# Side work in queued steps of one engine, and expert products in 16-bit parts

## The chip, the cores and the metric

The kernel runs on one core of a Trainium2 chip. A core has five engines with a queue of instructions each: TensorE (PE, with its weight loads shown apart as PEld), VectorE (DVE), ScalarE (ACT), GpSimd (POOL) and SyncE (SP, which here issues DMA transfers). An engine takes its instructions in order; between engines, semaphores order the work. Matrix products land in PSUM, which DVE and ACT can read; POOL works in SBUF.

The metric is the device time of one execution in microseconds. Before the change it is 1541.74 us, the median of three runs (1539.69 to 1550.02).

## The reference

Four layers run one after the other on x of shape (2, 1024, 128), each normalised and added to a residual stream. The first two are the ones that change. The first is attention with 8 heads; the second routes each token to 2 of 8 experts and adds a shared expert:

```python
Q = (x @ Wq.T).reshape(b, n, H, R)            # H = 8, R = 64
K = (x @ Wk.T).reshape(b, n, H, R)
V = (x @ Wv.T).reshape(b, n, H, d)            # d = 128
attn = softmax(einsum('bnhr,bmhr->bhnm', Q, K))
out = einsum('bhnm,bmhd->bnd', attn, V)       # summed over heads
...
scores = softmax(xt @ gate_w.T)
top_vals, idx = top_k(scores, 2)
xs = xt[:, None, :] * weights[:, :, None]     # the token times its score
for e in range(8):
    mask = (idx == e)
    h  = silu(xs @ w1[e].T + b1[e])
    x2 = h @ w2[e].T + b2[e]
    x3 = xs @ w3[e].T + b3[e]
    y  = y + sum(x2 * x3 * mask)
z = silu(xt @ sw1.T) * (xt @ sw2.T) @ sw3.T   # shared, inner size 256
return y + z
```

The third layer is attention with 16 heads and a linear position bias, the fourth two layers of windowed attention with feed-forward parts. The kernel computes every expert for every token; the score of an expert that a token did not choose is zero.

## The kernel before

**Precision.** A product of float32 operands is made from two parts of each operand, a high one (the value rounded to a shorter type) and a low one (the rest). Three products of parts replace one (`mm3`, lines 48 to 50): high × high, high × low, low × high. The first layer uses float16 parts, the expert stage float32r parts.

**First stage** (`phase1`, from line 177). Eight pairs (two batches, four pairs of heads) of 16 steps each make 128 steps, and the loop over m runs them. A step computes scores of 128 keys for 512 queries and two heads (L300, 8 matmuls into a PSUM tile `big`), their exponentials on ACT (L304), the high part on ACT (L306) and the low part on POOL (L307). Row maxima are computed 12 steps ahead: a matmul (L269) and a reduction on DVE (L272). Nine steps behind, `values` multiplies the exponentials of eight steps with V (24 matmuls, L48 to L50) into one of two PSUM tiles in turn, `pu` and `sm`, and one step later `accumulate` divides and adds on DVE (L328, L331, L333). Every 16 steps the next pair's projections, with parts on ACT and DVE (L157/L158, L214/L215), go in between.

**Order of the work.** `queue(f)` issues a piece of work behind the last instruction recorded on each engine, so that queued work runs in the order of the program; a scheduler orders what is not queued. The main pieces of the first stage are queued. Preparation for a later stage is written as a generator; `tick()` runs it to its next `yield`. In the first stage it is called at m = 72, 76, 82, 86, 92 and at every second m from 101. One such step uses several engines, among them: loading and splitting the expert weights (ACT L429, POOL L430), `biases` with a transfer of b3 (L507 to L513), normalising the tokens (`ln_stats` on DVE with a power on POOL, L80 to L87; applied on ACT, L116), transposing them (PE L164), and `gates` (softmax of the gate, ranks, scores, L458 to L499).

**Expert stage** (`phase2`, from line 403). For each batch come two halves of the shared expert (e = −2, −1), then eight experts: 20 units over 1024 tokens each, with the channels on partitions. `stage_a` multiplies the transposed tokens with the scores, which a DMA of 512 KB broadcasts to all partitions (`fetch`), and splits the result (DVE L556, ACT L558, POOL L559). `stage_b` makes the first and third products (one matmul per 512 tokens with the bias b3 as an outer product with the mask, L580), silu on ACT (L575), and splits h (ACT L582, DVE L583). `stage_c` makes the second product, y = (p + b2) · x3 on DVE (L600) and adds it to yT on DVE or POOL in turn (L601). None of these is queued. Three PSUM tiles `big` of two banks are shared by all products. `finish` transposes yT back, normalises and adds it to X (L609, L610). From i = 13 two ticks per unit prepare the third stage.

```python
if m in (72, 76, 82, 86, 92) or m >= 101 and m % 2 == 0:
    k.queue(k.tick)
```

Of the kernel before, what the change touches and what calls it, by code (L numbers as in the profile page):

```python
# [22 lines left out]
NT = N // 128  # L23
# [6 lines left out]
class Core:  # L30


    def __init__(self, tc, A):
        self.tc, self.nc, self.A = tc, tc.nc, A
        self.last = {}

# [100 lines left out]
    def add_ln_steps(self, pool, X, src, T, t0):  # L137

        mv, rstd = self.ln_stats(pool, src, T)
        yield  # L140
        y = pool.tile([128, T, D], F32, name="ln_y")
        self.ln_to(pool, [y[:, t, :] for t in range(T)], src, mv, rstd, True)
        yield
        self.nc.vector.tensor_tensor(X[:, t0 : t0 + T, :], X[:, t0 : t0 + T, :], y, ALU.add)
# [32 lines left out]
def phase1(k, X):  # L177
# [9 lines left out]
    with ExitStack() as es:  # L187
# [31 lines left out]
        def tokens(b):  # L219
            xn = tp.tile([128, NT, D], F32, name="xn")  # L220
            xTh, xTl = x2.tile([128, N], F16, name="xTh"), x2.tile([128, N], F16, name="xTl")
            for c in range(2):
                src = X[:, NT * b + 4 * c : NT * b + 4 * c + 4, :]
                mv, rstd = k.ln_stats(x2, lambda t: src[:, t, :], 4, False)
                yield
                k.ln_to(x2, [xn[:, 4 * c + t, :] for t in range(4)], lambda t: src[:, t, :], mv, rstd, scalar=b == 1)
                s = slice(512 * c, 512 * c + 512)
                yield
                hi, _ = k.split_r(xTh[:, s], xTl[:, s], k.transposed(ps_sm, xn, c))
                S["first"] = S.get("first", hi)  # L230
            S["x", b] = xTh, xTl

# [77 lines left out]
        def values(n):  # L310
# [4 lines left out]

            S["u", n] = po = ps_u.tile([128, D + 1], F32, name="pu") if n % 2 else ps_sm.tile([128, D + 1], F32, name="sm")
# [5 lines left out]
        def accumulate(n):  # L322
# [11 lines left out]
            if h == H - 1 and i == 7:  # L334
                args = X, lambda t: acc[:, 4 * c + t, :], 4, NT * b + 4 * c
                if b == 0 or c == 0:
                    S["finish"] = k.add_ln_steps(xp, *args)
                else:
                    k.later.append(lambda pool: k.add_ln(pool, *args, scalar=True))
# [21 lines left out]
        for m in range(steps + lag + 1):  # L361
# [8 lines left out]
            if m == 100:  # L370
                projecting.close()
# [3 lines left out]
            if 0 <= m - lag - 1 < steps:  # L375
                k.queue(accumulate, m - lag - 1)
            if "finish" in S and m % 2:
                k.queue(next, S["finish"], None)
            if 0 <= m - lag < steps:
                k.queue(values, m - lag)  # L380
            if m % 8 == 4 and m + 4 < steps:
# [3 lines left out]
            if m == 22:  # L385
                more = tokens(1)
            if m in (22, 26, 30, 36, 42):
                k.queue(next, more, None)
# [4 lines left out]
            if m in (72, 76, 82, 86, 92) or m >= 101 and m % 2 == 0:  # L393
                k.queue(k.tick)


def np_halves(w):

    v = w.rearrange("p t d -> p (t d)")
    return [v[:, 512 * i : 512 * i + 512].rearrange("p (t d) -> p t d", d=64) for i in range(2)]  # L400


def phase2(k, X):

    nc, A = k.nc, k.A
    E = 8
    with ExitStack() as es:
        pool = lambda name, bufs: es.enter_context(k.pool(name, bufs, "right"))
        sp = pool("p2s", 1)
        gp = pool("p2g", 1)  # L410
        dp = es.enter_context(k.tc.tile_pool(name="p2d", bufs=2, space=bass.MemoryType.DRAM))
# [3 lines left out]
        work = lambda: gp.tile([128, NT, 128], F32, name="work")  # L415
# [5 lines left out]
        b2 = lambda e: gb[:, 2 * E + e : 2 * E + e + 1]  # L421
        W = {}

        def load(pool, n, m, raw, split=nc.vector):
            w = raw[:, :m, :]
            nc.sync.dma_start(w, A["t_" + n])
            yield
            h, l = pool.tile([128, m, D], F32R, name=n + "h"), pool.tile([128, m, D], F32R, name=n + "l")
            nc.scalar.copy(h, w)  # L429
            split.tensor_tensor(l, w, k.f(h), ALU.subtract)  # L430
            W[n] = h, l

        S = {}

        def tokens(b, xp):

            Xb = X[:, NT * b : NT * b + NT, :]
            mv, rstd = k.ln_stats(gp, lambda t: Xb[:, t, :])
            yield
            xn = work()  # L440
            xT = xp.tile([128, N], F32, name="xT")
            xTh = xp.tile([128, N], F32R, name="xTh")
            xTl = xp.tile([128, N], F32R, name="xTl")
            S[b] = xT, xTh, xTl
            k.ln_to(gp, [xn[:, t, :] for t in range(NT)], lambda t: Xb[:, t, :], mv, rstd, scalar=True)
            yield
            for c in range(2):
                s = slice(512 * c, 512 * c + 512)
                ps = k.transposed(ps_sm, xn, c)
                nc.scalar.copy(xT[:, s], ps)  # L450
                k.split_r(xTh[:, s], xTl[:, s], xT[:, s])
                yield

        def gates(b, xp):
# [3 lines left out]
            for t in range(NT):  # L458
                nc.tensor.matmul(ps[:, t, :], xT[:, 128 * t : 128 * t + 128], gwT, start=True, stop=True)
            m = gp.tile([128, NT], F32, name="m")  # L460
# [3 lines left out]
            nc.vector.tensor_tensor(lg, ps, bc(m), ALU.subtract)  # L464
            ex = gp.tile([128, NT, E], F32, name="ex")
# [7 lines left out]
            cmp, c2 = (work_.rearrange("p t (i e) -> p t i e", e=E) for work_ in np_halves(work()))  # L473
            mine = sc.unsqueeze(3).to_broadcast([128, NT, E, E])
            other = sc.unsqueeze(2).to_broadcast([128, NT, E, E])
            nc.vector.tensor_tensor(cmp, other, mine, ALU.is_gt)
            nc.vector.tensor_tensor(c2, other, mine, ALU.is_equal)
            yield
            nc.vector.tensor_tensor(c2, c2, k.tri.unsqueeze(1).to_broadcast([128, NT, E, E]), ALU.mult)
            nc.vector.tensor_tensor(cmp, cmp, c2, ALU.add)  # L480
            rank = gp.tile([128, NT, E], F32, name="rank")
            nc.vector.tensor_reduce(rank, cmp, AX.X, ALU.add)
            rows = work()
            nc.gpsimd.memset(rows, 0.0)
            for o in (0, 32):
                nc.vector.tensor_scalar(rows[:, :, o : o + E], rank, 1.5, None, ALU.is_lt)
            nc.vector.tensor_tensor(rows[:, :, 64 : 64 + E], sc, rows[:, :, 0:E], ALU.mult)
            yield
            rT = xp.tile([128, N], F32R, name="rT")
            sT = gp.tile([128, N], F32, name="sT")  # L490
            for c in range(2):
                s = slice(512 * c, 512 * c + 512)
                ps = k.transposed(ps_sm, rows, c)
                nc.scalar.copy(rT[0:64, s], ps[0:64, :])
                nc.scalar.copy(sT[64 : 64 + E, s], ps[64 : 64 + E, :])
                yield
            sd = dp.tile([E, N], F32, name="sd")
            nc.sync.dma_start(sd, sT[64 : 64 + E, :])
            S[b] += rT, sd  # L499


        b3n = sp.tile([128, D], F32, name="b3n")
        b3r = sp.tile([128, D], F32R, name="b3r")
        b3s = sp.tile([128, E, D], F32R, name="b3s")

        def biases():
            nc.gpsimd.memset(b3n, 0.0)  # L507
            nc.sync.dma_start(b3n[0:E, :], A["L0_ffn_b3"])
            nc.sync.dma_start(b3n[32 : 32 + E, :], A["L0_ffn_b3"])
            nc.vector.tensor_copy(b3r, b3n)  # L510
            nc.vector.tensor_tensor(b3r[32:64, :], b3n[32:64, :], k.f(b3r[32:64, :]), ALU.subtract)
            bc = lambda ap, d: ap.unsqueeze(d).to_broadcast([128, E, D])
            nc.vector.tensor_tensor(b3s, bc(k.f(b3r), 1), bc(k.bsel, 2), ALU.mult)  # L513

        for n in ("sw", "w1", "w3"):
            yield from load(sp, n, 6 if n == "sw" else E, work(), nc.gpsimd)
            yield
        biases()
        x0 = pool("p2x", 1)
        yield  # L520
# [7 lines left out]
        op = pool("p2o", 2)  # L528
        wp = pool("p2w", 1)
        x1 = pool("p2y", 1)  # L530
        def outs(b):
            S[b] += (xp.tile([128, N], F32, name="yT"),)

        wl = lambda n, i: (W[n][0][:, i, :], W[n][1][:, i, :])

        def product(ps, w, hi, lo, start=True):
            for c in range(2):
                s = slice(512 * c, 512 * c + 512)
                k.mm3(ps[:, c, :], *w, hi[:, s], lo[:, s], start=start)
# [4 lines left out]
        def fetch(b, e):  # L544
            if e >= 0:
                sb = tile_of("sb")
# [3 lines left out]
        def stage_a(b, e):  # L550
            xT, xTh, xTl = S[b][:3]
            if e < 0:
                S["x", b, e] = xTh, xTl
                return
            xs = tile_of("xs")
            nc.vector.tensor_tensor(xs, xT, S.pop(("s", b, e)), ALU.mult)  # L556
            xh, xl = tile_of("xh", F32R, bufs=3), tile_of("xl", F32R, bufs=3)
            nc.scalar.copy(xh, xs)  # L558
            S["xl"] = nc.gpsimd.tensor_tensor(xl, xs, k.f(xh), ALU.subtract)  # L559
            S["x", b, e] = xh, xl  # L560

        def stage_b(b, e):
            xh, xl = S.pop(("x", b, e))
            p1, p3 = big(), big()
            h = tile_of("h")
            hh, hl = tile_of("hh", F32R), tile_of("hl", F32R)
            x3 = tile_of("x3")
            if e < 0:
                product(p1, wl("sw", e + 2), xh, xl)
                S["silu"] = nc.scalar.activation(x3, flat(p1), AF.Silu)  # L570
                product(p3, wl("sw", e + 4), xh, xl)
                nc.vector.tensor_tensor(h, flat(p3), x3, ALU.mult)
            else:
# [1007 lines left out]
```

## Time and profile before

| | |
|---|---|
| median of three runs | 1541.74 us (1539.69 to 1550.02) |
| the profiled execution, its own time | 1537.82 us |
| its span in the profile | 1536.0 us |
| first stage, first to last exponential | 31.1 to 454.12 us |
| last accumulation of the first stage ends | 473.04 us |
| expert stage, last addition to yT ends | 626.86 us |
| first row maximum of the third stage | 649.2 us |
| DVE busy in the expert stage, 475 to 627 us | 138 of 152 us |
| mean granted TensorE clock | 0.899 |

All times within the execution count from the start of its span. The page gives the busy time of each engine and the costliest groups of instructions: line and engine, the names written and read with their shapes, how often, then busy time and mean duration, then the idle time of the engine just before them and what ended it ("releaser"). An idle time is put down to the event that came last. The span is 1.8 us shorter than the execution's own time. A matmul's record is longer than its share of the engine's time, since matmuls overlap.

### The profile page before, as it was taken

The page shows a single profiled execution, that of the slowest core. Times are in us where ns is not written, and L with a number is a line of the kernel's source. Part 1 is how long each engine was busy: PE and PEld are TensorE (multiplying, and loading weights), DVE is VectorE, ACT ScalarE, POOL GpSimd, SP SyncE. Part 2 cuts the span into 40 slices and gives each one's busy share as a digit, 9 for nine tenths or more (in the row PEclk, how much of TensorE's full clock was granted, in tenths as well). Part 3 has the DMA queues.
Part 4 walks back from the last instruction along what each step waited for, and adds up shares of the span by engine and source line. Part 5 has one row for each costly group of instructions (what it writes and reads, how often), then busy time and mean ns, then how long its engine had stood idle before and what let it go on. Part 6 is the DMA issues. An engine that isn't in the chain of part 4 may idle for free.

```text
span 1536.0 us, 28795 instructions
## 1 busy us (share of the span) xinstructions
PE 1229.4 (80%) x11579; PEld 785.4 (51%) x11579; DVE 1135.5 (74%) x2159; ACT 951.1 (62%) x1405; POOL 882.6 (57%) x523
## 2 busy tenths in 40 slices
PE   4899999997887887688998578864778779668785
PEld 1466665665665654444544244432555556445564
DVE  6676667766647899797888968485869669569755
ACT  2877787776755755158787558952456446456544
POOL 1766666676564456436766837674656566446521
PEclk7999999999998989689999889985889889889897
DMA  2000000000002030000001010014686745546641
GB/s 68 1 1 2 1 2 1 15 16 2 1 16 96 15 106 33 7 3 5 4 5 35 18 48 6 1 18 92 109 141 125 143 83 109 103 81 121 130 77 40
DMA packets 178433, 72.27 MB, mean 47 GB/s; under 512 B 160091, under 2 KB 169323, under 8 KB 178299
## 3 DMA queue, kind: packets, MB, share of 16 engines
q1 hardware_dynamic: 176395, 69.15, 21.7%
q8 instruction: 91, 1.49, 0.4%
q10 hardware_dynamic: 1472, 1.09, 0.2%
q0 software_dynamic: 432, 0.20, 0.1%
q14 instruction: 43, 0.35, 0.1%
HBM read 21.64 MB, written 2.16 MB: 15 GB/s over the span
## 4 chain that ended last, share of the span: by engine, by line
DVE 38%; PE 34%; ACT 11%; DMA 7%; issue 5%; POOL 3%; SPq 2%; POOLq 0%; DVEq 0%; ACTq 0%
DVE mx L806 6%; PE big L300 4%; DVE nm L272 3%; PE sm L48 2%; PE pu L857 2%; PE sm L50 2%; PE sm L49 2%; ACT pt L835 2%; DVE X L153 2%; DMA oT<-o 1%; DMA hc<-X 1%; DVE ln_st L80 1%; DMA hx<-X 1%; PE pu L48 1%; DVE ss L1133 1%
## 5 line engine op out<-in xcount | busy, mean ns | idle before, releaser
L307 POOL TENSOR_TENSOR hl<-p,hl 128x1024 f16<-128x1024 f32 x128 | 272.4, 2133 | 155.7 <-ACT hl L306 139.7
L840 POOL TENSOR_TENSOR hl<-pt,hl 128x2048 f16<-128x2048 f32 (+1 forms) x48 | 165.0, 3444 | 99.2 <-ACT hl L839 58.8
L272 DVE TENSOR_REDUCE nm<-big 128x2 f32<-128x1024 f32 x128 | 155.3, 1221 | 47.2 <-PE big L269 47.0
L304 ACT ACTIVATE p<-big 128x1024 f32<-128x1024 f32 x128 | 131.1, 1024 | 54.1 <-PE big L300 53.1
L306 ACT CAST hl<-p 128x1024 f16<-128x1024 f32 x128 | 134.0, 1047 | 4.0
L1131 POOL TENSOR_TENSOR rot<-rot,t 128x512 f32<-128x512 f32 x64 | 85.3, 1337 | 78.2 <-DVE t L1125 45.2
L48 PEld LDWEIGHTS <-hl 128*128 128x128 f16 x1024 | 100.4, 98 | 56.7 <-issue 46.7
L806 DVE TENSOR_REDUCE mx<-bankz 128x1 f16<-128x512 f32 (+3 forms) x156 | 100.0, 660 | 33.9 <-PE bankz L801 25.7
L835 ACT ACTIVATE pt<-bank 128x512 f32<-128x512 f32 (+1 forms) x173 | 97.6, 605 | 40.5 <-PE bank L834 27.6
L87 POOL TENSOR_TENSOR ln_rstd<-ln_rs,nhalf 128x4 f32<-128x4 f32 (+2 forms) x36 | 45.8, 1276 | 107.7 <-DVE ln_rs L83 87.9
L49 PEld LDWEIGHTS <-hl 128*128 128x128 f16 x1024 | 101.1, 99 | 12.6 <-issue 11.5
L806 DVE TENSOR_REDUCE mx<-bank 128x1 f16<-128x512 f32 (+1 forms) x148 | 94.6, 657 | 14.3 <-PE bank L801 10.2
L50 PEld LDWEIGHTS <-hl 128*128 128x128 f16 x1024 | 100.3, 98 | 0.0
L835 ACT ACTIVATE pt<-bankz 128x512 f32<-128x512 f32 (+1 forms) x131 | 75.4, 601 | 28.3 <-PE bankz L834 21.3
L832 PE MATMUL bank<-qst,kz 128*128 128x512 f16 (+3 forms) x222 | 66.6, 341 | 27.0 <-DVE mx L806 23.7
L839 ACT CAST hl<-pt 128x2048 f16<-128x2048 f32 (+1 forms) x48 | 78.8, 1641 | 13.0 <-PE pu L857 12.9
L1151 POOL TENSOR_TENSOR rot<-rot,rn 128x512 f32<-128x512 f32 x64 | 69.2, 1101 | 12.7 <-DVE rn L1141 11.4
L1249 ACT ACTIVATE p<-b 128x512 f32<-128x512 f32 x64 | 37.7, 599 | 54.5 <-PE b L1248 54.1
L1278 POOL TENSOR_TENSOR o<-u,o 128x512 f16<-128x512 f32 x32 | 39.0, 1218 | 55.9 <-DVE o L1096 28.1
L797 PE MATMUL bank<-kz,qst 128*128 128x512 f16 (+3 forms) x170 | 58.7, 364 | 11.6 <-DVE mx L806 8.3
L797 PE MATMUL bankz<-kz,qst 128*128 128x512 f16 (+3 forms) x214 | 63.1, 335 | 5.8 <-DVE mx L806 3.4
L797 PEld LDWEIGHTS <-qst 128*128 128x128 f16 x384 | 38.0, 102 | 50.1 <-issue 35.1
(417 smaller groups left out, 4439.4 us busy)
## 6 DMA issues: line engine op xcount, KB each, us to landing
sb<-sd SPq DMA_DIRECT2D x16, 512.0 KB
Vs<-V SPq DMA_DIRECT2D x56, 130.0 KB
work<-in_t_w SPq DMA_DIRECT2D x3, 512.0 KB
kept<-X SPq DMA_DIRECT2D x2, 512.0 KB
hx<-X SPq DMA_DIRECT2D x8, 128.0 KB
hx<-X SPq DMA_DIRECT2D x8, 127.0 KB
out<-X SPq DMA_DIRECT2D x3, 256.0 KB
hc<-X SPq DMA_DIRECT2D x5, 128.0 KB
```

The source lines that it names most:

```text
L48: mm(out, lh, rh, start=start, stop=False, **kw)
L49: mm(out, lh, rl, start=False, stop=False, **kw)
L50: mm(out, ll, rh, start=False, stop=stop, **kw)
L272: S["red"] = nc.vector.tensor_reduce(S["n", u][:, i // 2, c, :], ps, AX.X, ALU.max, negate=True)
L304: S["exp"] = nc.scalar.activation(p, st, AF.Exp, scale=QSCALE**-2)
L306: nc.scalar.copy(hl[:, 0], p)
L307: S["lo"] = nc.gpsimd.tensor_tensor(hl[:, 1], p, hl[:, 0], ALU.subtract)
L797: nc.tensor.matmul(ps[:, a, :n], q0[:, 128 * t : 128 * t + 128], kz[:, a0 + a, 512 * e : 512 * e + n], start=True, stop=not diag)
L806: S["max"] = nc.vector.tensor_reduce(out, ps[:, :, :n], AX.X, ALU.max, negate=True)
L835: S["exp"] = nc.scalar.activation(pt[:, a0 : a0 + m, :w], st[:, :, :w], AF.Exp)
L840: nc.gpsimd.tensor_tensor(hl[:, 1, :, :w], pt[:, :, :w], hl[:, 0, :, :w], ALU.subtract)
L1131: eng("ra" if j else "rb", i).tensor_tensor(rot[:, j], rot[:, j], t2[:, j], ALU.add)
```

## The change

**Side work.** The class gets a list `side` of generators. `aside(n)` takes the first of them and runs n of its steps, each queued. Normalisation (`ln_steps`), transposition (`transposed_steps`) and the gates are written so that a step uses one engine as far as possible; the power of the normalisation stays on POOL and its application goes to ACT throughout. In the first stage one step of `side` runs per m, and a tick only where `side` is empty, for 80 <= m < 89 and from 101. Values always use the PSUM tile `pu`, and the accumulation follows them at once; the loop is one step shorter.

**Expert stage.** Weights and tokens are split into float16 parts, the weights scaled by 64. The tokens are not multiplied with the score; the first and third products are, after the matmuls, by DVE (`first`, `third`). This changes what the bias terms mean, so an expert that a token did not choose leaves (w2 · silu(b1) + b2) · b3 in the sum, which a correction takes off: `constants` works it out per expert, and one float32 product of it with the mask `nT` of the experts not chosen is added to the shared expert's product. b3 is added by ACT with the scale (`scaled`). The low part of h goes to POOL, the sum of y to POOL but for two experts. Batch 0 takes its routed experts first and the shared halves last; batch 1 the shared halves first. All of it is queued.

```diff
+    def aside(self, n=1):
+        while n and self.side:
+            if self.queue(next, self.side[0], self) is self:
+                self.side.pop(0)
+            n -= 1
+
+    def ln_steps(self, pool, dst, src, per=2):
+        nc, T = self.nc, len(dst)
+        st = pool.tile([128, T, 6], F32, name="ln_st")
+        mv = pool.tile([128, T, 2], F32, name="ln_mv")
+        for t in range(T):
+            nc.vector.bn_stats(st[:, t, :], src(t))
+            nc.vector.bn_aggr(mv[:, t, :], st[:, t, :])
+            if t % per == per - 1 and t < T - 1:
+                yield
+        rs = pool.tile([128, T], F32, name="ln_rs")
+        nc.vector.tensor_scalar(rs, mv[:, :, 1], EPS, None, ALU.add)
         yield
+        rstd = pool.tile([128, T], F32, name="ln_rstd")
+        nc.gpsimd.tensor_tensor(rstd, rs, self.nhalf[:, :T], ALU.pow)
+        yield
+        nb = pool.tile([128, T], F32, name="ln_nb")
+        nc.vector.scalar_tensor_tensor(nb, mv[:, :, 0], -1.0, rstd, ALU.mult, ALU.mult)
+        yield
+        for t, y in enumerate(dst):
+            nc.scalar.activation(y, src(t), AF.Identity, scale=rstd[:, t : t + 1], bias=nb[:, t : t + 1])
+            if t % per == per - 1:
+                yield
...
-            S["u", n] = po = ps_u.tile([128, D + 1], F32, name="pu") if n % 2 else ps_sm.tile([128, D + 1], F32, name="sm")
+            S["u", n] = po = ps_u.tile([128, D + 1], F32, name="pu")
...
-            if 0 <= m - lag - 1 < steps:
-                k.queue(accumulate, m - lag - 1)
-            if "finish" in S and m % 2:
-                k.queue(next, S["finish"], None)
             if 0 <= m - lag < steps:
                 k.queue(values, m - lag)
+                k.queue(accumulate, m - lag)
...
-            if m in (72, 76, 82, 86, 92) or m >= 101 and m % 2 == 0:
+            if k.side:
+                k.aside()
+            elif 80 <= m < 89 or m >= 101:
                 k.queue(k.tick)
...
+        def parts(n, m, w):
+            h, l = sp.tile([128, m, D], F16, name=n + "h"), sp.tile([128, m, D], F16, name=n + "l")
+            nc.scalar.activation(h, w, AF.Copy, scale=WS)
+            yield
+            nc.vector.scalar_tensor_tensor(l, w, WS, h, ALU.mult, ALU.subtract)
...
+        def first(b, e):
+            p = big()
+            product(p, wl("w1", e) if e < E else wl("sw", e - E), *S[b][1:3])
+            h = tile_of("h", bufs=3)
+            if e < E:
+                nc.vector.tensor_tensor(h, flat(p), S["s", b, e], ALU.mult)
+                silu = nc.scalar.activation(h, h, AF.Silu, bias=b1(e), scale=1 / WS)
...
+                split(b, e, h, nc.gpsimd)
...
+        def third(b, e):
+            p = big()
+            product(p, wl("w3", e) if e < E else wl("sw", e - E + 2), *S[b][1:3])
+            if e < E:
+                x3 = tile_of("x3", bufs=3)
+                nc.vector.tensor_tensor(x3, flat(p), S.pop(("s", b, e)), ALU.mult)
...
+            if e == E:
                 for c in range(2):
+                    nc.tensor.matmul(p[:, c, :], S["c"], S[b][3][:, 512 * c : 512 * c + 512], start=True, stop=False)
...
+            y = yT if start else tile_of("y")
+            nc.vector.scalar_tensor_tensor(y, flat(p), bs[:, 0, e : e + 1], S.pop(("x3", b, e)), ALU.add, ALU.mult)
+            if not start:
+                S["add"] = lambda: (nc.vector if e in (4, E - 1) else nc.gpsimd).tensor_tensor(yT, yT, y, ALU.add)
...
+        units = [(0, e) for e in range(E + 2)] + [(1, e) for e in (E, E + 1, *range(E))]
...
+        k.side += [f(xp) for f in k.later]
+        k.later.clear()
+        k.side += [tokens(1, x1), gates(1, x1)]
+        k.side.insert(1, constants())
+        for i in range(-3, n + 3):
...
             if 0 <= i < n:
+                k.queue(first, *units[i])
+            k.queue(pending, "split")
             if 0 <= i - 1 < n:
+                k.queue(scaled, *units[i - 1])
+                if units[i - 1][1] >= E:
+                    k.queue(pending, "split")
+            k.queue(pending, "add")
+            if i >= 0:
+                k.aside(3 if i < 7 else 2)
+            if 0 <= i - 2 < n:
+                k.queue(second, *units[i - 2])
+            if 0 <= i < n:
+                k.queue(third, *units[i])
+            if 0 <= i + 3 < n:
+                k.queue(fetch, *units[i + 3])
+            if i >= 0:
+                k.aside(2)
...
+                    k.side.append(finish(b))
+            if i >= 14:
+                k.queue(k.tick)
+                k.queue(k.tick)
+        while k.side:
+            k.aside()
```

## The prediction

> **What bounds the kernel now.** I read the page first, then the starts of the exponentials in the timeline, then the waits, the groups by form and the windows of the two stages that change. The page:
>
> ```profile
> span 1536.0 us, 28795 instructions
> PE 1229.4 (80%) x11579; PEld 785.4 (51%) x11579; DVE 1135.5 (74%) x2159; ACT 951.1 (62%) x1405; POOL 882.6 (57%) x523
> L307 POOL TENSOR_TENSOR hl<-p,hl 128x1024 f16<-128x1024 f32 x128 | 272.4, 2133 | 155.7 <-ACT hl L306 139.7
> L272 DVE TENSOR_REDUCE nm<-big 128x2 f32<-128x1024 f32 x128 | 155.3, 1221 | 47.2 <-PE big L269 47.0
> ```
>
> The sums hide two stages with different limits. The windows (columns: busy us and instructions of PE, weight loads, DVE, ACT, POOL, then granted clock, DMA share, GB/s): the first stage, then the two batches of the expert stage.
>
> ```profile
> 31.00:473.00 442.00, 400.96 (x4727) 269.53 (x4722) 287.44 (x537) 325.66 (x347) 289.11 (x140) 0.98 0.02 5
> 475.00:549.00 74.00, 59.22 (x229) 41.10 (x229) 67.38 (x62) 49.94 (x61) 36.63 (x15) 0.91 0.15 53
> 549.00:627.00 78.00, 59.67 (x200) 39.29 (x201) 70.33 (x94) 39.85 (x44) 46.43 (x20) 0.87 0.23 71
> ```
>
> In the first stage PE sets the step: 2.67 us from one exponential to the next where nothing else runs. With its projections, a block of 16 steps undisturbed lasts 49.0 us (two of the eight blocks do). In the expert stage DVE is busy 90% of both batches, so there DVE is the bound. The exponentials, ACT's timeline (start, us, idle before, releaser):
>
> ```profile
> 369.59 1.02 ACT L304 ACTIVATE p<-big 128x1024 f32<-128x1024 f32 x1 [0.55 <-PE big L300]
> 381.27 1.03 ACT L304 ACTIVATE p<-big 128x1024 f32<-128x1024 f32 x1 [9.58 <-PE big L300]
> 383.92 1.02 ACT L304 ACTIVATE p<-big 128x1024 f32<-128x1024 f32 x1 [0.54 <-PE big L300]
> ...
> 401.17 1.02 ACT L304 ACTIVATE p<-big 128x1024 f32<-128x1024 f32 x1
> ...
> 405.96 1.02 ACT L304 ACTIVATE p<-big 128x1024 f32<-128x1024 f32 x1
> ```
>
> 383.92 − 381.27 is a plain step; 11.7 us lie before it, and 4.8 us (401.17 to 405.96) in a step with one tick of preparation. DVE's timeline and the waits (us in total, times, longest) say why:
>
> ```profile
> 371.82 0.29 DVE L510 CAST b3r<-b3n 128x128 fp32r<-128x128 f32 x1 [5.71 <-DMA b3n<-in_L_ffn_b]
> 372.20 2.05 DVE L511 TENSOR_TENSOR b3r<-b3n,b3r 32x128 fp32r<-32x128 f32 x1
> 374.28 1.22 DVE L513 TENSOR_TENSOR b3s<-b3r,bsel 128x1024 fp32r<-128x1024 f32 x1
> ```
>
> ```profile
> DVE b3r L510 <- DMA b3n<-in_L_ffn_b: 5.7, 1, 5.7
> PE pu L48 <- DVE acc L333: 16.4, 5, 7.5
> ```
>
> In an in-order queue DVE waits for a small transfer, the reductions (L272) and accumulations (L333) behind it are late, and PE runs out of buffers.
>
> **First stage.** The 127 intervals from the first exponential (31.1) to the last (454.12) sum to 423.0 us. Undisturbed they would be 7 × 49.0, and 37.6 for the last block, which has neither projections nor, from its fourth step, maxima: 380.6. So 42.4 us are stalls: 2.6, 2.8, 2.8, 0, 6.2, 0, 12.6 and 15.3 by block. The change hands out one step of one engine per m and drops b3's transfer. What is left, block by block, each an estimate: 4.6 and 2.2 (the second batch's tokens, now at m 12 to 48), 4.5 (the first normalised sum, 6.2 now), 4.1 (four weight subtractions go from POOL L430, 2.35 us, to DVE, 1.23 us each, against 0.97 to 0.99 us of idle per step, plus a port wait), 2 and 4 (gates in some 27 steps). That is 21.4. If only steps that meet the subtractions of a projection stall, about 9 remain. The ends are 0 and today's 42; I take 17. **−25.4.**
>
> Values now use one PSUM buffer with the accumulation right behind. PE must wait 0.04 + 0.56 + 0.05 us (values' end to reciprocal, reciprocal with L333, L333 to the next matmul) = 0.65. In the trace 1.11 us of scores and maxima lie between two sets of values, so a plain step has 0.46 us to spare: cost 0. In the last 9 steps nothing lies between: about 2.2 us each, where 18.9 us now pass from the last exponential to the last accumulation (473.04), with expert products among them. I reckon 21.5: **+2.6.**
>
> **Expert stage, work.** Now, by form between 475 and 640 (count, then busy, mean ns, idle before):
>
> ```profile
> L559 POOL TENSOR_TENSOR xl<-xs,xh 128x1024 fp32r<-128x1024 f32 x16 | 44.5, 2785 | 33.1 <-ACT xh L558 33.1
> L556 DVE TENSOR_TENSOR xs<-xT,sb 128x1024 f32<-128x1024 f32 x16 | 31.6, 1976 | 2.8 <-DMA sb<-sd 1.9 <-POOL xl L559 0.8
> L583 DVE TENSOR_TENSOR hl<-h,hh 128x1024 fp32r<-128x1024 f32 x20 | 30.5, 1527 | 4.2 <-ACT hh L582 4.2
> L600 DVE SCALAR_TENSOR_TENSOR y<-big,gb,x 128x1024 f32<-128x1024 f32 x16 | 20.4, 1275 | 2.9 <-PE big L50 2.8
> L601 DVE TENSOR_TENSOR yT<-yT,y 128x1024 f32<-128x1024 f32 x8 | 11.9, 1490 | 0.1
> ```
>
> Per routed unit DVE now does xs, hl, y and half an add: 1.98 + 1.53 + 1.28 + 0.75 = 5.5 us. After: three passes from PSUM (h and x3 like L572, 1.22 each, and y, 1.28) = 3.7, with adds on DVE for two experts of eight. PE: 20 products of about 0.23 become 18 of 0.216, 3.9 us. ACT: silu 1.11, cast 1.05, x3 1.01. POOL: a split like L307, 2.13, and mostly an add of 2.4 to 2.6 (L601 on POOL). So a unit's own work is about 4 us on every engine but ACT. Side work for DVE stays near 35 us; the whole stage's DVE sum falls from about 138 to about 105. That is the floor; 8 us of start make it 113. SP still issues sixteen score broadcasts of 512 KB, three units ahead; one lands within 3 us of its issue (487.89 to 490.5).
>
> The Trainium skill (GPSIMD Engine Reference, 4.1 Engine selection) speaks against this part: two-input elementwise work belongs on VectorE, since GpSimd is about twice as slow. The rows agree on the ratio, 1.14 to 1.21 us on DVE undisturbed and 2.13 on POOL; by the rule the 20 moved splits would cost 20 × 1.0 = 20 us, by the windows nothing while POOL, busy 83 of 152 us, stays under DVE.
>
> **Expert stage, order.** Everything is queued, so each engine runs in program order, and one iteration hands out up to five steps in two slots: three in a row between first and second product, two after the third. Three consecutive steps are one chain over two or three engines, which is what a tick is today. Its price is the tick row: 4.79 to 5.60 us instead of 2.67, 2.1 to 2.9; I take 2.2 a slot. Stages:
> - Start: before, shared experts need no scores and begin at 474.2, 1 us after 473.04. After, routed ones begin: transposed rows, copies, scores out (a small store, 1.8 us from issue at 547.17 to landing at 548.99), first broadcast (2.7): 8.0.
> - Units 0 to 6: 4.0 + 2 × 2.2 = 8.4 each, 58.8.
> - Units 7 to 13 (gates, shared experts, few side steps): 4.0 and one wait of 1.2, like DVE's 1.13 for POOL at L486; 7 × 5.2 = 36.4.
> - Units 14 to 19, two ticks of the third stage each (its weight loads among them): 5 intervals of 8.4 = 42.0.
> - Two more iterations to the last yT: 9.0.
>
> Sum 154.2; now 473.04 to 626.86, 153.8: **+0.4.** Adding every wait in the built order in series gives 170 (+16). Ends: 113 (−41) and 195 (+41, the slower rival). The −33 of DVE work are thus spent on queues. The correction for unselected tokens is in the side steps, but for two fp32 products of 512 columns per batch: some 0.44 us each by the 0.109 of a 128-column fp32 transposition, under 2 us in all.
>
> **Behind it.** From 626.86 to the third stage's first maximum, 649.2, are 22.3 us. The closing normalisation becomes chains PE, ACT, DVE, POOL, DVE, ACT, DVE per half: **+2**, ends −4 and +8. Later stages keep their code; their order may move by a few us either way. I put 0.
>
> The granted clock is 0.98 over the first stage and 0.74 in 620–640, where PE is busy 9.4 of 20 us. At 0.8 the 3.9 us of a unit's products become 4.9, still below 8.4, so the clock adds nothing.
>
> The Trainium skill (TensorE: Matmul & The Clock Gate, The HAM clock gate) would give half speed after an idle window of some 3.4 us: 7.8 us of products per unit, and up to +4 for each unit stalled so long, some 50 us over twelve if nothing overlaps. The rows here show 0.74 as the lowest mean over 20 us, so I don't count it.
>
> **Sum:** −25.4 + 2.6 + 0.4 + 2 = −20.4. The profiled execution took 1537.82 us, 3.9 less than the median of the runs, 1541.74. Against itself 1517.4; for a median I forecast 1521.
>
> **Rivals.**
> - *Waits overlap* (chance 0.19). Three PSUM buffers let DVE's queue stay ahead; units cost about 6 instead of 8.4, 12 × 2.4 = 29 less: 1541.7 − 20.4 − 28.8 = 1493. For it: x and x3 hold three buffers each. Against: DVE's order is fixed.
> - *The fine steps don't help the first stage* (0.14). One PSUM buffer with 0.46 us to spare, and DVE side steps held by POOL: the column reduction to fp16, L281, took 2.06 us at 273.29 where others of its size take 0.2. Some 40 such steps × 0.6 = 24 eat the gain: 1545. Against: POOL leaves about 0.5 us per step, and both accumulation and maxima read PSUM at 0.35 and 1.22 beside it.
> - *Slower: DVE held behind POOL's split* (0.25). In units 0 to 6 and 14 to 18 the bias step of a normalisation on DVE waits for POOL's power, which is queued behind the split: silu 1.11 + cast 1.05 + split 2.13 + power 1.0 = 5.3 us, with h, x3 and y queued behind and PE out of buffers. Unit: 4.0 + 5.3 + 2.2 = 11.5, plus 0.3 where the split is contended (2.28): 12 × 3.4 = 41, total +20, 1562. It decides for slower than 1% once these units pass 11.4 us. For it: L556 and L583 already vary with POOL. Against: not every unit's slot holds such a step.
>
> **Numbers.** Forecast 0.42 (within 9 us of 1521, so 0.33 of it beyond 1%), rivals as given. A run here can tell about 1% (15 us) from no change. Faster: 0.33 + 0.19 = 0.52; same: 0.09 + 0.12 = 0.21; slower: 0.25 + 0.02 = 0.27. The range reaches from the first rival to just past the last, 1493 to 1566.
>
> **What would show it.** Right: no interval of exponentials over 6 us, the last one at about 429 and the last accumulation near 450; first expert product's h on DVE some 8 us later; h to h 8 to 9 us in units 0 to 6; DVE busy well under 90% there. Wrong: intervals of 3.3 throughout (second rival), h to h at 6 (first) or beyond 11 with DVE waiting for POOL's power (third), or a later stage that moves by over 10 us, which I have not priced.

## The result and the profile after

The changed kernel takes 1560.61 us (median of four runs, 1558.71 to 1562.33); the kernel before, with one more run, 1542.9 (four runs, 1539.69 to 1550.02). The ratio is 1.0108 with a 95% interval of 1.0070 to 1.0146: slower by 1.1%, where 1.3% faster was forecast. The profiled execution has a span of 1560.5 us, 24.5 more than the one before; it took 1562.33 us, the longest of its kernel's four runs, and the one before 1537.82, less than any of the four, so the stages below add up to more than the medians differ.

| us in the profiled executions | before | after | difference | forecast |
|---|---|---|---|---|
| first to last exponential | 31.1 to 454.1 | 31.3 to 432.4 | −22.0 | −25.4 |
| to the end of the last accumulation | 473.0 | 458.1 | +6.8 | +2.6 |
| expert stage, to the last yT | 153.8 | 187.8 | +34.0 | +0.4 |
| to the third stage's first maximum | 22.3 | 25.3 | +3.0 | +2 |
| from there to the end | 886.8 | 889.3 | +2.5 | 0 |

The page of the kernel after, its head and the line that answers to L307:

```profile
span 1560.5 us, 28792 instructions
PE 1210.3 (78%) x11580; PEld 744.3 (48%) x11580; DVE 1097.3 (70%) x2147; ACT 943.1 (60%) x1410; POOL 873.8 (56%) x530
L351 POOL TENSOR_TENSOR hl<-p,hl 128x1024 f16<-128x1024 f32 x128 | 273.7, 2141 | 147.2 <-ACT hl L350 118.3
```

Every compute engine is busy for a shorter time, and the kernel takes longer. ACT's timeline of the kernel after, around the place where 11.7 us lay between two exponentials before (step 106):

```profile
371.83 1.00 ACT L348 ACTIVATE p<-big 128x1024 f32<-128x1024 f32 x1
374.78 1.02 ACT L348 ACTIVATE p<-big 128x1024 f32<-128x1024 f32 x1
377.43 1.02 ACT L348 ACTIVATE p<-big 128x1024 f32<-128x1024 f32 x1 [0.55 <-PE big L344]
380.33 1.02 ACT L348 ACTIVATE p<-big 128x1024 f32<-128x1024 f32 x1 [0.31 <-PE big L344]
```

The intervals are 2.95, 2.65 and 2.90 us, where they were 11.7, 2.65 and 5.6; no interval exceeds 6.3 us. The first stage gave nearly what was forecast. The windows of the expert stage (span, then busy us and instructions of PE, weight loads, DVE, ACT, POOL, granted clock, DMA share, GB/s), first the whole stage of the kernel before:

```profile
473.04:626.86 153.82, 119.66 (x432) 80.67 (x430) 139.64 (x164) 89.65 (x104) 83.68 (x34) 0.89 0.19 63
```

and of the kernel after: start, units 0 to 6, 7 to 13, 14 to 18 (each from silu to silu), and the end.

```profile
458.05:468.40 10.35, 3.74 (x20) 1.81 (x19) 1.29 (x3) 2.45 (x4) 0.00 (x0) 0.90 0.58 181
468.40:540.00 71.60, 33.36 (x156) 15.49 (x156) 33.10 (x67) 31.88 (x43) 27.17 (x15) 0.71 0.11 40
540.00:581.30 41.30, 38.02 (x158) 16.39 (x157) 26.26 (x29) 22.43 (x27) 20.42 (x10) 0.94 0.20 65
581.30:634.20 52.90, 29.44 (x99) 11.09 (x99) 31.75 (x61) 20.29 (x27) 22.21 (x12) 0.81 0.13 38
634.20:645.86 11.66, 6.04 (x18) 2.61 (x19) 7.29 (x6) 5.64 (x5) 7.79 (x4) 0.76 0.09 23
```

DVE's work fell from 139.6 to 99.7 us (the five rows sum to it). In units 0 to 6, 10.2 us each, no engine is busy half the time; in units 14 to 18, 10.6 us each, none is busy for more than about 60%. Between them, where few side steps stand, a unit takes 5.9 us. The waits of DVE in the whole stage (us in total, times, longest):

```profile
DVE ln_nb L162 <- POOL ln_rstd L159: 13.8, 5, 4.7
DVE y L662 <- PE big L51: 11.0, 5, 3.8
DVE h L624 <- DMA sb<-sd: 9.1, 1, 9.1
DVE X L173 <- ACT ln_y L165: 5.7, 3, 4.9
DVE rank L532 <- POOL cmp L529: 5.5, 1, 5.5
DVE xTl L184 <- ACT xT L182: 4.3, 1, 4.3
```

Apart from one wait of 9.1 us for the first scores, at the start, these are many small waits of different kinds, ahead of a side step or of a product that PE made late. One of them in full, from the timelines of ACT, POOL and DVE:

```profile
498.48 1.13 ACT L625 ACTIVATE h<-h,gb 128x1024 f32<-128x1024 f32 x1
499.64 1.04 ACT L616 CAST hh<-h 128x1024 f16<-128x1024 f32 x1
```

```profile
500.82 2.12 POOL L617 TENSOR_TENSOR hl<-h,hh 128x1024 f16<-128x1024 f32 x1 [4.14 <-ACT hh L616]
502.90 1.00 POOL L159 TENSOR_TENSOR ln_rstd<-ln_rs,nhalf 128x4 f32<-128x4 f32 x1
```

```profile
499.12 0.17 DVE L156 TENSOR_SCALAR ln_rs<-ln_mv 128x4 f32<-128x4 f32 x1
503.94 0.16 DVE L162 SCALAR_TENSOR_TENSOR ln_nb<-ln_mv,ln_rstd 128x4 f32<-128x4 f32 x1 [4.65 <-POOL ln_rstd L159]
504.03 1.28 DVE L662 SCALAR_TENSOR_TENSOR y<-big,bs,x 128x1024 f32<-128x1024 f32 x1
505.23 1.22 DVE L638 TENSOR_TENSOR x<-big,sb 128x1024 f32<-128x1024 f32 x1
506.37 1.22 DVE L624 TENSOR_TENSOR h<-big,sb 128x1024 f32<-128x1024 f32 x1
```

A power of 1.00 us stands behind POOL's split, which waits for ACT's cast, which waits for silu. DVE is done with `ln_rs` at 499.3 and stands 4.65 us in front of `ln_nb`, with y, x3 and the next h behind it, from products that PE had finished by 500.3.

### The profile page after: what moved, and what is told of

Read it like the earlier page. It is cut to its first block, busy times and chain, and to the rows that moved or that the text cites. A ratio compares the mean times of both kernels' runs of the same rounds, so it can differ in the third digit from the quotient of the medians.

```text
span 1560.5 us, 28792 instructions
## 1 busy us (share of the span) xinstructions
PE 1210.3 (78%) x11580; PEld 744.3 (48%) x11580; DVE 1097.3 (70%) x2147; ACT 943.1 (60%) x1410; POOL 873.8 (56%) x530
## 4 chain that ended last, share of the span: by engine, by line
PE 35%; DVE 33%; ACT 11%; DMA 8%; issue 6%; POOL 4%; SPq 3%; POOLq 0%; DVEq 0%; ACTq 0%
DVE mx L893 6%; PE big L344 3%; PE pu L49 3%; DVE nm L316 3%; PE pu L51 3%; PE pu L50 3%; DMA oT<-o 2%; PE pu L944 2%; ACT pt L922 2%; SPq L1104 2%; PE big L49 2%; PE big L51 2%; PE big L50 2%; DMA hc<-X 2%; DVE ss L1220 1%
## 5 line engine op out<-in xcount | busy, mean ns | idle before, releaser
L617 POOL TENSOR_TENSOR hl<-h,hh 128x1024 f16<-128x1024 f32 x20 | 42.5, 2128 | 108.8 <-ACT hh L616 90.5
L49 PE MATMUL pu<-V1h,hl 128*128 128x129 f16 x512 | 92.6, 224 | 12.5 <-DVE acc L376 11.7
L49 PE MATMUL pu<-V0h,hl 128*128 128x129 f16 x512 | 91.9, 223 | 6.5 <-DVE acc L374 3.4
L51 PE MATMUL pu<-V1h,hl 128*128 128x129 f16 x512 | 92.0, 222 | 0.0
L50 PE MATMUL pu<-V1l,hl 128*128 128x129 f16 x512 | 92.0, 221 | 0.0
L51 PE MATMUL pu<-V0h,hl 128*128 128x129 f16 x512 | 91.3, 221 | 0.0
L50 PE MATMUL pu<-V0l,hl 128*128 128x129 f16 x512 | 91.3, 220 | 0.0
```

The costliest lines, as they stand in the source:

```text
L49: mm(out, lh, rh, start=start, stop=False, **kw)
L50: mm(out, lh, rl, start=False, stop=False, **kw)
L51: mm(out, ll, rh, start=False, stop=stop, **kw)
```

## The experiments

All kernels here leave the fourth stage out (the local attention and feed-forward layers), so their times stand against runs of the same three stages: 1023.36 us for the changed kernel, 1006.38 for the one before. The first two stages' instructions and their order are untouched by that. Stage times come from one profile each; each kernel here was run once. The control, and the kernel before over three stages, show how far two profiles of the same work differ: by 0.9 and about 3 us.

**Control: the changed kernel, three stages.**

> The changed kernel without its fourth stage (the local attention and feed-forward layers are left out, here and in all runs that follow; the instructions of the first two stages are the same in the same order). A control: last accumulation at 458, units 0 to 6 of the expert stage 10.2 us each, last yT at 646, third stage's first maximum at 671, each within 2 us.

Last accumulation 458.35, last yT 645.0, first maximum 670.8, units 0 to 6 10.1 us each. As in the full kernel, within 0.9 us.

**Only the first stage changed.** The loop of the changed `phase1`, with `phase2` and the tick times of before. Against the changed loop:

```diff
             if k.side:
                 k.aside()
-            elif 80 <= m < 89 or m >= 101:
+            if m in (72, 76, 82, 86, 92) or m >= 101 and m % 2 == 0:
                 k.queue(k.tick)
```

> The changed first stage's loop (one PSUM buffer for values, accumulation right behind, normalisation and tokens of the second batch as side steps) with the expert stage of before and its preparation of several engines per step, at the m of before. Theory A, the first stage's gain of 15 us lies in the preparation's steps: the intervals of 11.7 us come back, last accumulation at 470 to 480 us, the third stage's first maximum at 648 to 657. Rival, the gain lies in the loop's own order: last accumulation at 462 or earlier, first maximum at 630 to 638.

The intervals of 12.5 and 10.6 us are back at steps 106 and 120, the last accumulation ends at 475.84, first maximum at 652.5: theory A. ACT's timeline and DVE's wait in this kernel:

```profile
366.85 1.02 ACT L348 ACTIVATE p<-big 128x1024 f32<-128x1024 f32 x1 [0.55 <-PE big L344]
379.38 1.02 ACT L348 ACTIVATE p<-big 128x1024 f32<-128x1024 f32 x1 [10.44 <-PE big L344]
```

```profile
DVE b3r L554 <- DMA b3n<-in_L_ffn_b: 5.5, 1, 5.5
```

From the first exponential to the last it takes 419.4 us, where the kernel before takes 423.0 and the changed one 401.1: 18 of the 22 us lie in the preparation's steps, under 4 in the loop's own order. Part of that is b3's transfer, as DVE's wait shows; what the other changes of the steps give (one engine per step, other times) this run does not tell apart.

**No side steps in batch 0 of the expert stage.**

```diff
-        k.side += [f(xp) for f in k.later]
         k.later.clear()
-        k.side += [tokens(1, x1), gates(1, x1)]
-        k.side.insert(1, constants())
+        S[1] = S[0][:5]
+        S["c"] = sp.tile([E, 128], F32, name="cT")
+        nc.gpsimd.memset(S["c"], 0.0)
```

> Without any side step in batch 0 of the expert stage. Left out: the last normalised sum of the attention, the tokens and gates of batch 1 (it takes those of batch 0) and the correction's values (zeros). Theory A, chains of side steps in the in-order queues cost the time: units 0 to 6 fall from 10.2 us to 4.5 to 5.5 each, last yT 35 us earlier, near 611. Rival B, only POOL's power behind its split: 14 us earlier. Rival C, the order of the main work itself is slow: units stay above 8 us, last yT under 15 us earlier.

Units 0 to 6 take 4.1 us each (468.7 to 497.2), last yT at 602.6, 42 us earlier. The order of the main work is sound, and a unit's own work is what the prediction had worked out. Some 40 queued side steps cost 42 us, their own work included.

**The steps spread over an iteration.** One step in each of five places (four from the eighth unit on):

```diff
                 k.queue(first, *units[i])
+            if 0 <= i < 7:
+                k.aside(1)
             k.queue(pending, "split")
...
+            if i >= 0:
+                k.aside(1)
             k.queue(pending, "add")
             if i >= 0:
-                k.aside(3 if i < 7 else 2)
+                k.aside(1)
             if 0 <= i - 2 < n:
                 k.queue(second, *units[i - 2])
+            if i >= 0:
+                k.aside(1)
...
             if i >= 0:
-                k.aside(2)
+                k.aside(1)
```

> The same side steps, one in each of four or five places of an iteration (behind the first product, the scaling, the addition, the second product, the third) instead of three and two in a row. Theory A: a step's result is mostly ready before the next one is reached; units 0 to 6 fall to 7 to 8 us, last yT 15 to 22 us earlier. Rival B: 4 to 8 us earlier, since the power still stands behind a split. Rival C: no change.

A miss: 9.9 us per unit, for 10.1 in the control, and last yT at 652.6, 7.6 us later. About half of that is in the mark: the edit also puts the first step of the closing `finish` ahead of the last addition to yT, which waits 5.0 us behind it (so that the transposition reads a sum without the last expert). The last y ends at 646.4, where the control has 642.8, 3.6 us later, and the own time is 3.7 us longer. Standing three in a row was not what made the steps dear. My reading, which this run alone does not show: a step is behind its engine's main work of that unit wherever it is put, and the next step, on another engine, waits for it with that engine's main work behind. Theory A was changed to that (A2 below).

**Side steps ahead of the split.**

```diff
                 k.queue(first, *units[i])
+            if i >= 0:
+                k.aside(3 if i < 7 else 2)
             k.queue(pending, "split")
...
-            if i >= 0:
-                k.aside(3 if i < 7 else 2)
```

> The three side steps in a row go ahead of POOL's split and ACT's scaling instead of behind them. Theory B, the power behind the split is the main wait: DVE's five waits for the power (13.8 us) fall to about 1.3 each, last yT (645.0 in the control) 8 to 12 us earlier. Theory A2, any step on another engine stands behind that engine's work for the same unit, wherever it is put: the wait moves to ACT's results or to the late split, last yT within 5 us of the control.

DVE's waits of the expert stage here:

```profile
DVE y L662 <- PE big L51: 13.1, 6, 3.8
DVE X L173 <- ACT ln_y L165: 8.6, 5, 3.8
DVE yT L664 <- PE sm L681: 6.1, 1, 6.1
DVE ln_nb L162 <- POOL ln_rstd L159: 5.6, 5, 1.1
```

The five waits for the power fall from 13.8 to 5.6 us, while those for ACT's normalised rows and for PE grow. Last yT comes at 639.1, 5.9 us earlier, but this mark hides part of the gain: as in the run before, the closing `finish` begins ahead of the last addition, and the third line is the wait of that addition for its transposition, which the control does not have. The last y ends at 631.8, 11.0 us earlier, the third stage's first maximum comes at 660.9, 9.9 us earlier, and the own time is 8.5 us shorter. That is theory B's 8 to 12 us and not A2's limit of 5: the split in front of the power was a real wait. It is also no more than a part of the loss: units 0 to 6 still take 9.2 us.

**Side steps not queued.** `aside` draws them at the same places, but they are left to the scheduler:

```diff
-    def aside(self, n=1):
+    def aside(self, n=1, free=False):
...
-            if self.queue(next, self.side[0], self) is self:
+            step = next(self.side[0], self) if free else self.queue(next, self.side[0], self)
+            if step is self:
...
-                k.aside(3 if i < 7 else 2)
+                k.aside(3 if i < 7 else 2, True)
...
-                k.aside(2)
+                k.aside(2, True)
```

> The side steps of the expert stage are drawn at the same places, but not queued: the scheduler orders their instructions among the main work, as it did before the change. Theory A2: DVE no longer waits in the middle of a chain, units 0 to 6 cost 6 to 7 us (4.1 without side work, and the side work's own 1.5 to 2 on DVE and PE), last yT 18 to 28 us earlier than 645.0. Rival C2, the side work itself is dear, 43 us of engine time in whatever order: within 8 us of 645.0.

Last yT at 596.5, 48.5 us earlier, more than twice what was expected at the middle and far beyond rival C2's 8; 4.7 us per unit in batch 0; 974.36 us for three stages. The side work's engine time is still there (DVE busy 104.6 us between 458.1 and 596.5), only its place differs. DVE's timeline of this kernel:

```profile
470.94 1.52 DVE L157 TENSOR_SCALAR ln_rs<-ln_mv 128x4 f32<-128x4 f32 x1
472.38 1.21 DVE L639 TENSOR_TENSOR x<-big,sb 128x1024 f32<-128x1024 f32 x1
473.51 1.21 DVE L625 TENSOR_TENSOR h<-big,sb 128x1024 f32<-128x1024 f32 x1
474.64 1.03 DVE L163 SCALAR_TENSOR_TENSOR ln_nb<-ln_mv,ln_rstd 128x4 f32<-128x4 f32 x1
```

Between `ln_rs` and `ln_nb` stand x3 and the next h, 2.3 us of main work, while POOL makes the power. Some steps were also moved ahead (the correction's silu ran at 9.7 us), which a later run tells apart.

**Only the third stage's ticks not queued.**

```diff
             if i >= 14:
-                k.queue(k.tick)
-                k.queue(k.tick)
+                k.tick()
+                k.tick()
```

> Only the third stage's preparation steps (two per unit from the fifteenth on) are not queued, as before the change. Theory A2: units 14 to 18, 10.6 us each in the control, fall to 7 to 8, last yT 12 to 18 us earlier than 645.0. Rival, the weights' transfers set these steps, in any order: within 4 us.

Units 14 to 18 fall from 10.5 to 8.1 us, last yT at 635.7, 9.3 us earlier: a real part, under the 12 to 18 expected. A wait of 4.88 us for the normalised rows of batch 0, a side step that is still queued, remains there.

**Two PSUM places for values.** Two halves of one PSUM tile in turn.

```diff
-            S["u", n] = po = ps_u.tile([128, D + 1], F32, name="pu")
+            S["u", n] = po = S["pus"][:, n % 2, : D + 1]
...
+        S["pus"] = ps_u.tile([128, 2, 256], F32, name="pu")
```

> Values alternate between two halves of one PSUM bank, the accumulation stays right behind. If the single buffer sets the tail: the nine steps after the last exponential fall from 2.2 to about 1.4 to 1.5 us each, last accumulation 6 to 8 us earlier than 458.35. The first 127 intervals change by under 3 us if a plain step has 0.46 us to spare, and fall by over 8 us if the buffer is what holds them.

Last accumulation at 458.26, and the tail's steps are still 2.2 us. PE still waits about 0.65 us for each accumulation, and the likely reason, which I did not test, is that the halves are one tile whose uses are ordered; so this says nothing on a second buffer. The kernel before has no such wait among the largest in its tail. The changed kernel has it, between 433 and 459:

```profile
PE pu L49 <- DVE acc L376: 8.1, 9, 3.3
```

**The kernel before, three stages.**

> The kernel before, without its fourth stage: the base for the times of the other runs over three stages. Last accumulation at 473, last yT at 627, third stage's first maximum at 649, each within 2 us; its own time near 1003 us, if the third stage lasts as long as behind the changed kernel (1023.4 there, with the first maximum at 670.8).

Last yT at 629.6, first maximum at 651.9, 1006.38 us. All events lie about 3 us later than in the full kernel, more than the 2 us expected.

**Neither side steps nor ticks queued in the expert stage.** The two edits together.

> The changed kernel with neither the expert stage's side steps nor the third stage's preparation queued there; the first stage stays queued. If the two waits are separate costs, both gains show: last yT 645.0 − 48.5 − 9.3 = 587, time near 966 and about 37 us below the kernel before. If the scheduler's freedom had been used up by the side steps: 594 to 598.

Last yT at 588.2, 968.26 us: 38 us (3.8%) below the kernel before and 55 below the changed one, over three stages. The two costs are separate. Units 14 to 18 take 6.5 us.

**Free steps, but none ahead of its unit.** Against the kernel with free steps, in both slots:

```diff
-                k.aside(2, True)
+                with k.tc.issue_after(S["silu"].ins):
+                    k.aside(2, True)
```

> Side steps not queued, but none may start ahead of the silu of the unit in whose iteration it is drawn. Theory A2, the room between the steps of a chain is what counts: last yT 600 to 612 (596.5 with free steps, 645.0 with queued ones). Rival D, the gain came from steps moved ahead, into the gap before the first unit and into the first stage: 625 or later.

Last yT at 608.4, units 0 to 6 at 4.7 us: theory A2. Room from the unit on gives 36.6 of the 48.5 us; moving steps ahead gives the other 12. These 12 do not lie in units 0 to 6, which take 4.7 us either way, but mostly in units 7 to 13: 7.1 us each here, 5.6 with steps wholly free.

**Only the correction's steps not queued.**

> Only the correction's six steps (silu and cast of b1, 24 narrow matmuls, a transposition) are not queued; the scheduler may place them anywhere. PE waited 19.4 us in all ahead of its first narrow matmul in the changed kernel, most of it in shadow of other waits. Theory A2: units 1 and 2 (9.2 and 13.8 us) lose one chain, and six steps fewer stand in the slots behind: last yT 8 to 14 us earlier than 645.0. Rival: the tokens' chain takes the slots and the time stays within 4 us.

Last yT at 642.7, 2.3 us earlier; units 0 to 6 still 10.4 us, as the rival says: the slots are taken by the steps behind. PE's wait of 19.4 us ahead of the narrow matmuls was in the shadow of the others.

## Why the prediction was wrong

**First stage: right but for the tail.** The intervals lost 22.0 us. My block-by-block sum of 21.4 us of stalls left over would have given −21.0; taking 17 instead went 3.4 us too far. The preparation's steps were the cause, as read, b3's transfer among them. The tail was under-sized: +6.8 for +2.6. The 2.2 us per step was right, but two of the tail's steps are longer (4.9 and 3.4 us). In the longer one a queued step of the gates stands ahead of the accumulation: DVE waits 1.82 us for POOL's `cmp`, then has 2.5 us of the gates' work, and PE waits 3.32 us for the accumulation behind. So queued steps, which my sum for the tail had put at nothing, cost time there as well.

**Work of a unit: right.** 4.0 us forecast, 4.1 measured without side steps; DVE's sum is 99.7 us, where 105 was forecast.

**Order of the expert stage: the step that failed.** I priced a slot at 2.2 us, by what a tick cost in the first stage, and came to 154.2 us; adding every wait in the built order in series gave 170. It took 187.8. Units 0 to 6 take 10.2 us with side steps and 4.1 without, so a slot there cost about 3 us; no run shows the 2.2 in this stage. Term by term: start 10.4 for 8.0, units 0 to 6 71.6 for 58.8, units 7 to 13 41.3 for 36.4, 14 to 18 52.9 for 42.0, the end 11.7 for 9.0. Every term was too low, the two with most side steps and ticks by most. The row was taken from a stage in which PE is the bound, maxima run 12 steps ahead and values nine steps behind; there, as I read it, a chain costs only what sticks out of that room. In the expert stage h, silu, split, y of one unit are themselves a chain, and a side step joins it on every engine. The sum in series, which I had put at the upper end, was too low itself.

**The slower rival had the size, not the cause.** It forecast 1562 from DVE held behind POOL's split and power, 11.5 us a unit. Those waits are there (13.8 us), but with the split out of their way only 8.5 us of the own time came back (11.0 up to the last y), about a third of the 34. That its number came out is luck: the other chains cost the rest.

**The clock: dismissed wrongly.** I took 0.74 over 20 us as the lowest and added nothing; the same table has 0.61, from 20 to 40 us. In the kernel after, PE runs dry in units 0 to 6 (the row above has 0.71). PE's timeline there, behind an idle stretch and then at full clock:

```profile
483.03 0.63 PE L50 MATMUL big<-xTl,w3h 128*128 128x512 f16 x1
483.46 0.63 PE L51 MATMUL big<-xTh,w3l 128*128 128x512 f16 x1
...
491.47 0.38 PE L50 MATMUL big<-xTl,w3h 128*128 128x512 f16 x1
491.68 0.38 PE L51 MATMUL big<-xTh,w3l 128*128 128x512 f16 x1
```

Starts are 0.43 us apart, then 0.21. Over the stage the clock's record has 74 of 188 us at half, 34 of 154 before. Counting matmuls 0.38 to 0.46 us apart, at 0.216 too much each, PE lost 15 us to it in the stage after and 7 before: about 8 of the 34 us can be the clock. I take it for a follower of the stalls, not their source: with free side steps the same products have 27 us at half clock. No run separates it. The Trainium skill's rule (TensorE: Matmul & The Clock Gate, The HAM clock gate), half speed after an idle window of 3.4 us, agrees with the long stalls: ahead of the one of 19.4 us just before these rows PE's last matmul ends at 461.79, the record goes to half at 466.23, and behind three other stalls of 6 us and more it does so 3.5 to 5.1 us after the last matmul. It also went to half at 609.59 and 619.83, where PE has no idle stretch over 3.1 us in the 5 us ahead. The bound of 50 us that I drew from the rule was far too high: it took twelve such stalls, and PE has five idle stretches over 3.4 us in the stage.

**GpSimd for splits.** The 20 us that the rule of the Trainium skill (GPSIMD Engine Reference, 4.1 Engine selection) gave for moving them to POOL did not show: without side steps a unit takes 4.1 us with the split on POOL, where 4.0 was forecast. No run has the split on DVE beside it.

**What stays open.** The 2.5 us behind the third stage's first maximum were not looked into, nor whether a true second PSUM bank would shorten the tail. The version without queues in the expert stage was run over three stages only; that its 38 us carry over to the whole kernel is not shown.

## What to carry to other kernels

Here a side step in an in-order queue cost a round trip, not its own duration, where the main work around it was itself a chain over the same engines: count the hops and where each one's engine stands, and trust that sum over a row from a stage with slack. Queued steps cost less in the stage whose main work runs many steps ahead; in the stage with a short chain the same steps cost 0.6 us a unit instead of 6 when a scheduler put main work between them. When every engine's busy time falls and the span grows, look for many small waits of different kinds as well as for one long one. And when an edit moves work, see that it does not move the mark that you measure by.

## What the runs showed of the hardware

A stall costs PE's clock as well: the granted clock is 0.50 over the 9.1 us of unit 0 of the changed kernel, in which PE has no matmul, and products that follow run 0.43 us apart instead of 0.21.

And DVE's work from SBUF alone can be held until POOL's operation ends. With the ticks not queued, eight normalising operations on DVE took 8.05 us; its timeline, then POOL's:

```profile
612.39 8.05 DVE L92 TENSOR_SCALAR work<-X,ln_mv,ln_rstd 128x128 f32<-128x128 f32 x8
```

```profile
612.56 2.39 POOL L664 TENSOR_TENSOR yT<-yT,y 128x1024 f32<-128x1024 f32 x1
614.91 2.13 POOL L617 TENSOR_TENSOR hl<-h,hh 128x1024 f16<-128x1024 f32 x1
616.99 2.35 POOL L664 TENSOR_TENSOR yT<-yT,y 128x1024 f32<-128x1024 f32 x1
```

Five of the eight take 0.34 us at most. The other three begin 0.05 to 0.08 us behind one of POOL's three operations and end 0.08 to 0.09 us behind its end, after 2.2 to 2.4 us. Eight of the same form took 2.13 us at 646.25 in the kernel before, with POOL idle. The same shows in the free steps above: `ln_rs` with 1.52 us and `ln_nb` with 1.03, 0.17 and 0.16 us elsewhere, end within 0.03 us of a split on POOL.
